# Local attention layers on one core: V shifted inside SBUF, key blocks paired by row half, a new order of the slot

## The chip, the cores and the metric

The kernel runs on one core of one Trainium2 chip. The metric is the device time in microseconds (us), as the median over runs; lower is better. Engines are named as in the profile: PE is TensorE's matmuls, PEld its weight loads, DVE is VectorE, ACT is ScalarE, POOL is GpSimd and SP is SyncE, whose queue issues the DMAs.

## The reference

Input `x` has 4 sequences of 512 tokens with 128 features. First comes one dense causal attention layer with 16 heads of 64, which the change leaves alone. Then a stack of 6 layers follows; each is local attention and a feed-forward part:

```python
def attn_layer(x, Wqkv, qs, ksc, Wo):
    q, k, v = split_heads(x @ Wqkv)          # 16 heads of 64
    q, k = l2norm(q) * qs, l2norm(k) * ksc   # t / max(|t|, 1e-12)
    q, k = rotary(q, scale), rotary(k, 1 / scale)
    out = local_attention(q, k, v)           # window 32
    return merge_heads(out) @ Wo
def local_attention(q, k, v):
    # tokens in blocks of 32; block j attends to key blocks j-1 and j, masked
    sim = einsum('bhwie,bhwje->bhwij', bq, bk2) * 8
    attn = softmax(where(mask, -max, sim), -1)
    return einsum('bhwij,bhwje->bhwie', attn, bv2)
def ffn_layer(x, g, bln, W1, b1, W2, b2):
    a, gate = split((layernorm(x, eps=1e-5) * g + bln) @ W1 + b1)
    return a * gelu(gate) @ W2 + b2
```

Each half of a layer takes the tokens with half of the features shifted by one token, and adds its result to `x`. So a query block of 32 tokens needs the keys and values of 64 tokens: its own block and the one before.

## The kernel before

The dense layer fills the first 571 us of the profiled execution. The 6 local layers are then cut into 96 units: 6 layers x 4 sequences x 4 tiles of 128 tokens (`NT` = 4). A unit has `NW` = 4 query blocks of `W` = 32 tokens. Heads are handled in pairs: `NC` = 8 pairs, and a pair is two heads h = 0, 1 of `HD` = 64.

The units are software pipelined. One call of `slot(n)` works on several of them: `u` is unit n (scores, softmax, attention times V), `prev` is unit n-1 (output projection and residual), `done` is unit n+1 (norms of q and k, their transposes, loading of V), `new` is unit n+2 (projection of k and of V, rotary products) and `newq` is unit n+3 (projection of q). All of it stands under `tc.manual_schedule()`: on each engine the instructions run in the order in which the functions are called, and semaphores are set between engines by what is read and written. The feed-forward part of a finished sequence is spread over the following slots by n modulo 4: type 0 has the hidden chunk 1 (`chunk`, L828 and L829), type 1 the mean of the layer norm (L100) and chunk 2, type 2 the variance (L109), the reciprocal root (`rsqrt`, L81 to L87) and the output `out` (L848), type 3 the scaling (L117), the affine step (L123, DVE) and chunk 0.

The order on PE in a slot before is: `scores` (L711 adds the mask band, L722 the products), `pair_sums` (L620), `project_out_2` (L784), the piece of the layer norm, the first half of k's projection (L547), `transpose_p` half 0 (L700), the second half of k's projection, `transpose_p` half 1, `times_v` halves 0 and 1 (L759), `project_v` (L562), the feed-forward chunk or output, q's projection (L547), and `transpose_o` (L700). DVE has `maximum` (L735), `guard` (L624), the two rotary products of q (L602, tiles `rot` and `t`), `residual` (L792), `sum_squares` of q (L596), then for each half of `times_v` the reciprocal L768 and the product L769, the transposes of q and k (L677, L685), the two rotary products of k (L602), `sum_squares` of k, and the gate of the chunk (L836). ACT has the exponentials (L743, 8 for each half), `seed` (L628, L629) between the halves, the copies of P's transposes (L703), `square` of k (L586), the copies of V (L569), gelu (L832) with the loading of its table, the loading of the first table again (L1005), `square` of q and the copies of `transpose_o` (L703). POOL has `newton`, `over_norm` (L640) and `add_rotated` (L614).

PSUM tiles: three of 2 banks each go round between the scores, the two halves of `times_v`, the projections of q and k, and the feed-forward chunk (`two_t`); two of one bank go round among the rest (`one_t`). The chunk takes the tile that half 1 of `times_v` had, so it waits for the product L769 that reads it.

A matmul here may use a part of the array: `scores` and `times_v` use tiles of 64 rows by 32 columns, so a pair of heads can take the upper and the lower row half at once, and four query blocks the four column groups. In the kernel before, row half h holds head h of the pair, and writes PSUM bank h; query block j writes the partitions 32j to 32j+31. For that, V of a head has to lie in the row half of its head, with the two key blocks of a query block side by side. So `project_v` stores V to DRAM (L574, `vd<-vt`), and two slots later `load_v` reads it back four times in that arrangement (L692, `vw<-vd`):

```python
rows = vd_rows(u, odd * W, P).rearrange("(j k) a x -> a k j x", k=2 * W)
...
    out=u.vw[c * HD : (c + 1) * HD, odd::2].rearrange("p j c d -> p j (c d)"), in_=rows[c]
```

Of the kernel before, what the change touches and what calls it, by code (L numbers as in the profile page):

```python
# [15 lines left out]
P = 128  # L16
# [16 lines left out]
def body(ctx: ExitStack, tc: tile.TileContext, a, out: bass.AP):  # L33
# [15 lines left out]
    small = ctx.enter_context(tc.tile_pool(name="small", bufs=4))  # L49
    dram = ctx.enter_context(tc.tile_pool(name="dram", bufs=1, space=bass.MemoryType.DRAM))  # L50
    def tmpt(n=S):
# [23 lines left out]
    def rsqrt(v, n, eng):  # L75
# [7 lines left out]
        for k in range(3):  # L83
# [3 lines left out]
            eng.tensor_tensor(y if k < 2 else v, y, t, ALU.mult)  # L87

    def layernorm_steps(state, bank, inT, outT, g=None, b=None, eng=nc.vector, nt=NT, temp=tmpt, later=None):

        w = nt * P

        def then(f):
            f() if later is None else later.append(f)

        def mean():
            m = bank()[:, 0:w]
            mm(m, lhsT=avg, rhs=inT(), start=True, stop=True)  # L100
            xc = state["xc"] = temp()[:, 0:w]
            nc.vector.tensor_tensor(xc, inT(), m, ALU.subtract)
            sq = state["sq"] = temp()[:, 0:w]
            then(lambda: nc.scalar.activation(sq, xc, AF.Square))

        def var():
            v = bank()
            for t in range(nt):
                mm(v[:, t : t + 1], lhsT=state["sq"][:, t * P : (t + 1) * P], rhs=avg[:, 0:1], start=True, stop=True)  # L109
            rs = state["rs"] = small.tile([P, NT], F32, tag="rs", name="rs")[:, 0:nt]  # L110
            nc.vector.tensor_scalar(rs, v[:, 0:nt], EPS, None, ALU.add)
            then(lambda: rsqrt(rs, nt, eng))

        def scale():
            bc = bank()[:, 0:w]
            for t in range(nt):
                nc.tensor.transpose(  # L117
                    bc[:, t * P : (t + 1) * P], state["rs"][:, t : t + 1].to_broadcast([P, P]), ident
                )
            h = state["h"] = outT()  # L120
            nc.vector.tensor_tensor(h, state["xc"], bc, ALU.mult)
            if g is not None:
                then(lambda: nc.vector.tensor_scalar(h, h, g, b, ALU.mult, ALU.add))  # L123

        return mean, var, scale
# [369 lines left out]
    ps = ctx.enter_context(tc.tile_pool(name="ps2", bufs=1, space=PSUM))  # L495
    s2a = ps2a = s2b = s2 = ps_one = vts = vds = None

# [60 lines left out]
    def project_v(u):  # L558
        vt = vts[u.n % 2]
        for g in range(2):  # L560
# [12 lines left out]
        used(u, 2)  # L573
        nc.sync.dma_start(out=vd_rows(u, W, P), in_=vt.rearrange("p a c d -> p a (c d)"))  # L574

    def vd_rows(u, first, n):
        r0 = u.T * P + first
        return vds[u.n // NT % 2][r0 : r0 + n]

# [74 lines left out]
    def second_step():  # L654

        nonlocal s2b, ps_one, vts, vds
        steps[1].close()
# [3 lines left out]

        vts = [s2b.tile([P, 2, NC, HD + 1], F32, tag=f"vt{j}", name=f"vt{j}") for j in range(2)]
        for t_ in vts:
            nc.gpsimd.memset(t_[:, :, :, HD : HD + 1], 1.0)
        vds = [dram.tile([W + S, 2, NC * (HD + 1)], F32, tag=f"vd{j}", name=f"vd{j}") for j in range(2)]
        for d_ in vds:
            nc.sync.dma_start(out=d_[0:W], in_=a["zeros"])

# [17 lines left out]

    def load_v(u):
        u.vw = s2b.tile([P, NW, NC, HD + 1], F32, tag="vw", name="vw", bufs=2)
        for odd in range(2):
            rows = vd_rows(u, odd * W, P).rearrange("(j k) a x -> a k j x", k=2 * W)  # L690
            for c in range(2):
                nc.sync.dma_start(  # L692
                    out=u.vw[c * HD : (c + 1) * HD, odd::2].rearrange("p j c d -> p j (c d)"), in_=rows[c]
                )

    def transposed(src, g, dst, col0):
# [6 lines left out]
        nc.scalar.copy(dst[:, 4 * g : 4 * g + 4, col0 : col0 + P], tp.rearrange("p (c t) -> p c t", c=4))  # L703

    def scores(u):

        sc = two_t(0, "ps_att")
        for j in range(NW):
            for h in range(2):
                rows = slice(h * HD, (h + 1) * HD)  # L710
                mm(  # L711
                    sc[j * W : (j + 1) * W, h, :],
                    lhsT=ident16[rows, h * HD : h * HD + W],
                    rhs=band[rows, min(u.T + j, 1)].unsqueeze(1).to_broadcast([HD, NC, 2 * W]),
                    start=True,
                    stop=False,
                    skip_group_check=True,
                )
        for c in range(NC):
            for j in range(NW):  # L720
                for h in range(2):
                    mm(  # L722
                        sc[j * W : (j + 1) * W, h, c * 2 * W : (c + 1) * 2 * W],
                        lhsT=u.qT[h * HD : (h + 1) * HD, j, c],
                        rhs=u.kT[h * HD : (h + 1) * HD, j : j + 2, c],
                        start=False,
                        stop=True,
                        skip_group_check=True,
                    )
        u.sc = sc  # L730
# [21 lines left out]
    def times_v(u, g):  # L752
        if g == 0:
            u.on = s2.tile([P, NC, 2, HD], F32, tag="on", name="on", bufs=1)
        o = two_t(g, "ps_att")
        for c in range(4):
            for j in range(NW):
                for h in range(2):
                    mm(  # L759
                        o[j * W : (j + 1) * W, h, c * (HD + 1) : (c + 1) * (HD + 1)],  # L760
                        lhsT=u.pT[h * HD : (h + 1) * HD, 4 * g + c, j * W : (j + 1) * W],
                        rhs=u.vw[h * HD : (h + 1) * HD, j, 4 * g + c, :],
                        start=True,
                        stop=True,
                    )
        ov = o[:, :, 0 : 4 * (HD + 1)].rearrange("p a (c d) -> p a c d", d=HD + 1)
        rden = small.tile([P, 2, 4, 1], F32, tag="rden", name="rden")
        nc.vector.reciprocal(rden, ov[:, :, :, HD : HD + 1])  # L768
        nc.vector.tensor_tensor(  # L769
            u.on[:, 4 * g : 4 * g + 4].rearrange("p c a d -> p a c d"),  # L770
            ov[:, :, :, 0:HD],
            rden.to_broadcast([P, 2, 4, HD]),
            ALU.mult,
        )

    def transpose_o(u):
        u.aT = s2.tile([P, NC, P], F32, tag="aT", name="aT", bufs=2)
        for g in range(2):
            transposed(u.on.rearrange("p c a d -> p (c a d)"), g, u.aT, 0)

    def project_out_2(u):
        y = u.y = one_t()
        for c in range(NC):
            mm(y[:, 0:P], lhsT=wo_w[0][:, c, :], rhs=u.aT[:, c, :], start=(c == 0), stop=(c == NC - 1))  # L784

# [140 lines left out]
    def slot(n, norm, move, geglu):  # L926
# [5 lines left out]
        if ends and new.T == 0:  # L932
            scales[0] = load_scales(new.i + 1)
        if done:
            load_v(done)
        if u:
            scores(u)
        if done:
            pair_sums(done)
        begin(unit(n + 4))  # L940
        if u:
            maximum(u)
        if done:
            guard(done)
        if u:
            exponents(u, 0)
        if done:
# [7 lines left out]
        if prev:  # L955
            project_out_2(prev)
            if prev.b + 1 == B and prev.T + 1 == NT and prev.i + 1 < L:
                wo_w[0] = load_wo(prev.i + 1)
        if new:
            rotate(new, 0, [lambda: residual(prev)] if prev else ())  # L960
        elif prev:
            residual(prev)
# [8 lines left out]
        if new:  # L971
            sum_squares(new, 0)
            add_rotated(new, 0)
            project(new, 1, k_tile, 0, 1)
        if u:
            transpose_p(u, 0)
        if new:
            project(new, 1, k_tile, 1)
        if u:
            transpose_p(u, 1)  # L980
        if new:
            square(new, 1)
        if u:
            times_v(u, 0)
            times_v(u, 1)
        while later:
            later.pop(0)()
        if done:
            transpose_q(done)
            transpose_k(done)  # L990
        if new:
            rotate(new, 1)
            add_rotated(new, 1)
            sum_squares(new, 1)
            project_v(new)
        if ends:
# [3 lines left out]
        if n == -1:  # L1000
            third_step()
        if newq:
            project(newq, 0, q_tile)
        if geglu and unit(n + 1):
            nc.scalar.preload_act_table_set("natural_log_exp_and_others")  # L1005
        if newq:
            square(newq, 0)
        if u:
            transpose_o(u)

# [108 lines left out]
def _constants(n):  # L1119
# [40 lines left out]
    ident16 = np.eye(P).astype(ml_dtypes.bfloat16)  # L1160
    zeros = np.zeros((W, 2, NC * (HD + 1)), f)
    return {"tabs": tabs, "band": band, "pen": pen, "ident16": ident16, "zeros": zeros, "pairs": pairs}
# [55 lines left out]
```

## Time and profile before

| | |
|---|---|
| median of 3 runs | 2262.44 us (2252.24 to 2264.42) |
| profiled execution: its own time | 2257.68 us |
| its span (first to last instruction) | 2255.9 us, mean granted PE clock 0.982 |
| dense layer / 96 slots and the end | 0 to 571 us / 571 to 2255.9 us |
| the 95 slots from the first to the last start | 571.0 to 2206.7 us, mean 17.2 us |
| busy: PE / DVE / ACT / POOL | 2108.4 / 1705.3 / 1457.2 / 1374.0 us |
| DMA: `vw<-vd` / `vd<-vt` | 384 of 260 KB / 96 of 520 KB |
| DMA of instructions (q8) | 309 packets, 5.06 MB |

A line of the page's groups reads: source line, engine, operation, output tile <- input tiles, shape, count, then busy time and mean duration in ns, and after the bar the idle time of the engine just before, with what ended most of it. "issue" stands for idle time in which the engine waited for nothing that the profile shows. In a timeline each row gives start and duration in us. The granted clock (PEclk) is 1.00 at full speed.

### The profile page before, as it was taken

How to read it: one execution, taken by the hardware profiler on the slowest of the kernel's cores; microseconds unless marked ns; L12 is line 12 of the kernel's file. 1: busy time of each engine (PE TensorE's matmuls, PEld its weight loads, DVE VectorE, ACT ScalarE, POOL GpSimd, SP SyncE). 2: the span in 40 equal slices, each digit the busy share in tenths (PEclk: the TensorE clock that was granted, in tenths of full speed). 3: DMA queues.
4: the chain of work that ended last, by engine and by line, in shares of the span. 5: the costliest groups of instructions: out<-in, count | busy, mean ns of one | idle time of the engine just before them, and what ended most of it. 6: DMA issues, size and time to landing. Idle time of an engine off the chain costs nothing.

```text
span 2255.9 us, 88566 instructions
## 1 busy us (share of the span) xinstructions
PE 2108.4 (93%) x39182; PEld 1338.7 (59%) x39182; DVE 1705.3 (76%) x2402; ACT 1457.2 (65%) x3860; POOL 1374.0 (61%) x1582
## 2 busy tenths in 40 slices
PE   7999999998898899989999999999889998999997
PEld 5655656554565556655566655666555665566665
DVE  4776767665787788877888877888778887878883
ACT  4665656664556667756677756777666776667763
POOL 2544545464666666766667666676666676666752
PEclk8999999999999999999999999999999999999998
DMA  3000000001343344333443424343343433434330
GB/s 122 1 1 1 1 1 1 1 1 29 88 117 88 89 124 118 93 92 89 125 117 106 109 82 117 103 116 99 98 114 98 116 99 98 114 89 115 101 101 23
DMA packets 88987, 180.35 MB, mean 80 GB/s; under 512 B 9342, under 2 KB 23548, under 8 KB 88572
## 3 DMA queue, kind: packets, MB, share of 16 engines
q1 hardware_dynamic: 87900, 172.98, 28.1%
q8 instruction: 309, 5.06, 1.0%
q10 hardware_dynamic: 704, 1.70, 0.2%
q14 instruction: 74, 0.61, 0.1%
HBM read 122.48 MB, written 52.43 MB: 78 GB/s over the span
## 4 chain that ended last, share of the span: by engine, by line
PE 78%; DVE 11%; ACT 5%; issue 4%; POOL 1%; DMA 0%; SPq 0%; DVEq 0%; ACTq 0%; POOLq 0%
PE ps_proj L547 13%; PE ps_one L700 7%; PE ps_one L784 6%; PE ps_att L759 6%; PE ps_att L722 6%; PE ps_one L562 6%; PE ps_sc L303 5%; PE ps_o L388 5%; PE ps_pt L368 4%; ACT pr L743 3%; PE ps_proj L828 3%; PE ps_proj L829 3%; DVE mx L735 2%; PE ps_att L711 1%; PE ps_proj L848 1%
## 5 line engine op out<-in xcount | busy, mean ns | idle before, releaser
L614 POOL TENSOR_TENSOR rot<-rot,t 128x1024 f32<-128x1024 f32 x192 | 457.4, 2382 | 225.6 <-DVE t L602 215.1
L743 ACT ACTIVATE pr<-ps_att,mx 128x64 f32<-128x64 f32 x1536 | 333.1, 328 | 202.9 <-DVE mx L735 202.9
L547 PE MATMUL ps_proj<-wqkv,xs 128*32 128x256 f32 x6144 | 399.3, 388 | 4.9 <-DVE t L602 2.5
L357 POOL TENSOR_TENSOR pr<-pr,den 128x1024 f32<-128x1024 f32 x128 | 240.9, 1893 | 248.1 <-DVE den L354 238.3
L640 POOL TENSOR_TENSOR rot<-rot,v 128x1024 f32<-128x1024 f32 x192 | 363.2, 1913 | 7.5
L547 PEld LDWEIGHTS ps_proj<-wqkv,xs 128*32 128x32 f32 x6144 | 172.5, 110 | 211.0 <-issue 120.0
L586 ACT ACTIVATE sq<-ps_proj 128x1024 f32<-128x1024 f32 x192 | 197.3, 1028 | 73.3 <-PE ps_proj L547 71.3
L602 DVE TENSOR_TENSOR t<-ps_proj,lt 128x1024 f32<-128x1024 f32 x192 | 232.4, 1210 | 0.0
L596 DVE TENSOR_REDUCE ss<-sq 128x32 f32<-128x1024 f32 x192 | 231.2, 1204 | 0.0
L602 DVE TENSOR_TENSOR rot<-ps_proj,lt 128x1024 f32<-128x1024 f32 x192 | 230.2, 1199 | 0.0
L569 ACT COPY vt<-ps_one 128x512 f32<-128x512 f32 x192 | 113.3, 590 | 180.7 <-PE ps_one L562 180.7
L343 ACT ACTIVATE pr<-ps_sc,nm 128x128 f32<-128x128 f32 (+3 forms) x448 | 220.3, 509 | 11.8 <-DVE nm L330 8.6
L784 PE MATMUL ps_one<-aT,wo 128*128 128x128 f32 x1536 | 201.8, 285 | 17.9 <-issue 17.7
L330 DVE TENSOR_REDUCE nm<-ps_sc 128x2 f32<-128x1024 f32 x128 | 156.0, 1219 | 64.4 <-PE ps_sc L318 64.4
L759 PE MATMUL ps_att<-vw,pT 64*32 64x65 f32 x12288 | 160.0, 225 | 44.2 <-issue 40.5
L784 PEld LDWEIGHTS ps_one<-aT,wo 128*128 128x128 f32 x1536 | 186.8, 198 | 19.6 <-issue 19.3
L562 PE MATMUL ps_one<-wqkv,xs 128*128 128x512 f32 x384 | 192.2, 622 | 6.5 <-DVE aT L398 3.6
L768 DVE RECIPROCAL rden<-ps_att 128x8 f32<-128x8 f32 x192 | 39.2, 204 | 203.0 <-PE ps_att L759 203.0
L759 PEld LDWEIGHTS ps_att<-vw,pT 64*32 64x32 f32 x12288 | 135.3, 105 | 70.3 <-issue 57.0
L634 POOL TENSOR_TENSOR yt<-y 128x64 f32<-128x64 f32 x96 | 28.0, 292 | 241.6 <-ACT y L629 239.7
L735 DVE TENSOR_REDUCE mx<-ps_att 128x16 f32<-128x1024 f32 x96 | 117.5, 1224 | 75.6 <-PE ps_att L722 75.2
L703 ACT COPY pT<-ps_one 128x512 f32<-128x512 f32 x192 | 114.8, 605 | 80.7 <-PE ps_one L700 80.6
(169 smaller groups left out, 3968.4 us busy)
## 6 DMA issues: line engine op xcount, KB each, us to landing
vw<-vd SPq DMA_DIRECT2D x384, 260.0 KB, 5.0
vd<-vt SPq DMA_DIRECT2D x96, 520.0 KB, 2.7
wqkv<-in_wqkv_dram SPq DMA_DIRECT2D x18, 512.0 KB, 3.8
wo<-in_wo_dram SPq DMA_DIRECT2D x6, 512.0 KB, 5.2
w<-in_w_dram SPq DMA_DIRECT2D x6, 341.0 KB, 3.5
xr<-in_x_dram SPq DMA_DIRECT2D x3, 256.0 KB
w<-in_w_dram SPq DMA_DIRECT2D x12, 64.0 KB
out_dram<-tmp_t SPq DMA_DIRECT2D x3, 256.0 KB, 2.3
```

Of the source, the lines that this page charges most:

```text
L343: nc.scalar.activation(self.pr[:, h, cols], self.sc[:, h, cols], AF.Exp, bias=self.nm[:, part_, h : h + 1], accum_out=self.den[:, part_, h ...
L357: nc.gpsimd.tensor_tensor(self.pr, self.pr, self.den[:, 0].unsqueeze(2).to_broadcast([P, 2, S]), ALU.mult)
L547: mm(u.p[j][b_ * W : (b_ + 1) * W, w_ // 2, w_ % 2 * n : (w_ % 2 + 1) * n], lhsT=u.xs[:, t0 : t0 + W], rhs=wpart[j][:, b_ * n : (b_ + 1) * n],
L562: mm(p, lhsT=u.xs[:, u.T * P : (u.T + 1) * P], rhs=wpart[2][:, g * 512 : (g + 1) * 512], start=True, stop=True,)
L586: nc.scalar.activation(u.sq[j], u.p[j], AF.Square)
L596: nc.vector.tensor_reduce(u.ss[:, j * GROUPS : (j + 1) * GROUPS], groups(u.sq[j]), AX.X, ALU.add)
L602: nc.vector.tensor_tensor(out_.rearrange("p (w c d) -> p w c d", w=NW, d=W), u.p[j].rearrange("p (w c d) -> p w c d", w=NW, d=W), lts[u.T] ...
L614: nc.gpsimd.tensor_tensor(r, r, t1[:, :, ::-1], ALU.add)
L640: nc.gpsimd.tensor_tensor(groups(u.r[j]), groups(u.r[j]), u.v[:, j * GROUPS : (j + 1) * GROUPS].unsqueeze(2).to_broadcast([P, GROUPS, W]), ...
L743: nc.scalar.activation(u.pr[:, c, h], u.sc[:, h, c * 2 * W : (c + 1) * 2 * W], AF.Exp, bias=u.mx[:, h, c : c + 1])
L759: mm(o[j * W : (j + 1) * W, h, c * (HD + 1) : (c + 1) * (HD + 1)], lhsT=u.pT[h * HD : (h + 1) * HD, 4 * g + c, j * W : (j + 1) * W], rhs=u ...
L784: mm(y[:, 0:P], lhsT=wo_w[0][:, c, :], rhs=u.aT[:, c, :], start=(c == 0), stop=(c == NC - 1))
```

## The change

Nothing changes in the dense layer or in the numbers of matmuls. In the local layers:

- **Key blocks by row half.** `PLACES` gives for each query block j and head h a bank `j // 2` and partitions `(h ^ j // 2) * 64 + j % 2 * 32`. In `scores` a row half still holds one head, but the two row halves now write the same bank, in different partitions. In `times_v` row half x holds the key blocks of the query blocks whose result goes to bank x, so that an odd block finds its two key blocks in `vt` as it was projected, and an even one in a copy `vs` that lies 32 tokens later.
- **V.** The store to DRAM and the four loads give way to two DMAs within SBUF (`shift_v`, 96 and 32 rows, 0.5 MB in all) into one buffer `vs`, issued after `times_v` of the slot. `vt` has three buffers instead of two.
- **Order.** k's projection is made whole, straight behind `scores`; q's projection comes last, behind `transpose_o`; ACT copies `transpose_o` before it squares q. On DVE the first rotary product of q moves ahead of `guard`, and the first rotary product of k moves ahead of the reciprocals of `times_v`, the second staying behind the transposes.
- **Layer norm in the slots.** The reciprocal root takes its first guess from ACT (Ln, then Exp) with one correction step on POOL, instead of two operations on DVE and three steps on POOL. The affine step moves from DVE to ACT.
- `wo`'s rows are permuted on the host side of the weights' layout to the new order of `on` and `aT`.

The core of the diff:

```diff
+    def rsqrt_log(v, n, eng):
...
+        nc.scalar.activation(y, v, AF.Ln)
+        nc.scalar.activation(y, y, AF.Exp, scale=-0.5)
+        eng.tensor_tensor(t, y, y, ALU.mult)
+        eng.tensor_tensor(t, t, v, ALU.mult)
+        eng.tensor_scalar(t, t, -0.5, 1.5, ALU.mult, ALU.add)
+        eng.tensor_tensor(v, y, t, ALU.mult)
...
-                then(lambda: nc.vector.tensor_scalar(h, h, g, b, ALU.mult, ALU.add))
...
+                    later.append(lambda: nc.scalar.activation(h, h, AF.Identity, bias=b, scale=g))
...
-        nc.sync.dma_start(out=vd_rows(u, W, P), in_=vt.rearrange("p a c d -> p a (c d)"))
...
+    def shift_v(u):
+        u.vs = s2b.tile([P, 2, NC, HD + 1], F32, tag="vs", name="vs")
+        nc.sync.dma_start(out=u.vs[W:P], in_=vts[u.n % 3][0 : P - W])
+        nc.sync.dma_start(out=u.vs[0:W], in_=vts[(u.n - 1) % 3][P - W : P] if u.T else a["zeros"])
...
+    PLACES = [(j, h, j // 2, (h ^ j // 2) * HD + j % 2 * W) for j in range(NW) for h in range(2)]
...
     def times_v(u, g):
...
+            for j, h, x_, p0 in sorted(PLACES, key=lambda f: (f[0] % 2, f[1], f[2])):
+                rows = slice(x_ * HD, (x_ + 1) * HD)
+                mm(
+                    o[p0 : p0 + W, x_, c * (HD + 1) : (c + 1) * (HD + 1)],
+                    lhsT=u.pT[rows, 4 * g + c, p0 : p0 + W],
+                    rhs=(vts[u.n % 3] if j % 2 else u.vs)[rows, h, 4 * g + c, :],
...
     def slot(n, norm, move, geglu):
...
-        if done:
-            load_v(done)
         if u:
             scores(u)
+        if new:
+            project(new, 1, k_tile)
         if done:
             pair_sums(done)
         begin(unit(n + 4))
         if u:
             maximum(u)
+            exponents(u, 0)
+        if new:
+            rotate(new, 0, [lambda: guard(done)] if done else ())
+        elif done:
             guard(done)
-        if u:
-            exponents(u, 0)
...
             sum_squares(new, 0)
             add_rotated(new, 0)
-            project(new, 1, k_tile, 0, 1)
         if u:
             transpose_p(u, 0)
-        if new:
-            project(new, 1, k_tile, 1)
-        if u:
             transpose_p(u, 1)
         if new:
             square(new, 1)
+        between = []
         if u:
-            times_v(u, 0)
-            times_v(u, 1)
...
+            between = [lambda: times_v(u, 0), lambda: times_v(u, 1)]
+        between.append(lambda: [f() for f in later] and later.clear())
         if done:
-            transpose_q(done)
-            transpose_k(done)
+            between.append(lambda: shift_v(done))
+            between.append(lambda: transpose_q(done))
+            between.append(lambda: transpose_k(done))
         if new:
-            rotate(new, 1)
+            rotate(new, 1, between)
             add_rotated(new, 1)
             sum_squares(new, 1)
...
+        if u:
+            transpose_o(u)
         if newq:
             project(newq, 0, q_tile)
...
             square(newq, 0)
-        if u:
-            transpose_o(u)
```

## The prediction

> **What bounds the kernel now.** I read the page first: engines, DMA queues, chain.
>
> ```profile
> PE 2108.4 (93%) x39182; PEld 1338.7 (59%) x39182; DVE 1705.3 (76%) x2402; ACT 1457.2 (65%) x3860; POOL 1374.0 (61%) x1582
> q1 hardware_dynamic: 87900, 172.98, 28.1%
> q8 instruction: 309, 5.06, 1.0%
> PE 78%; DVE 11%; ACT 5%; issue 4%; POOL 1%; DMA 0%; SPq 0%; DVEq 0%; ACTq 0%; POOLq 0%
> ```
>
> PE is busy for 93% and carries 78% of the chain. The DMA has 0% of the chain: the trip of V through DRAM (most of q1) is on no path by itself. Second, the waits:
>
> ```profile
> DVE rden L768 <- PE ps_att L759: 203.0, 130, 5.3
> PE ps_att L759 <- issue: 40.5, 34, 1.7
> PE ps_att L711 <- DVE t L602: 21.9, 19, 4.0
> PE ps_one L784 <- issue: 17.7, 10, 3.1
> PE ps_proj L828 <- DVE hT L123: 7.4, 10, 1.0
> ```
>
> PE hardly waits for data: 21.9 us at a slot's start for k's second rotary product, 7.4 for the affine step. Larger are the stalls with nothing to wait for. Third, one such stall in windows (PE, PEld, DVE, ACT and POOL busy, then clock, DMA share, GB/s):
>
> ```profile
> 1291.50:1295.00 3.50, 3.50 (x153) 3.29 (x152) 2.46 (x5) 1.68 (x5) 1.68 (x1) 1.00 0.93 211
> 1295.00:1297.20 2.20, 0.46 (x5) 0.27 (x3) 1.00 (x1) 2.17 (x12) 0.17 (x1) 1.00 0.73 149
> 1297.20:1300.00 2.80, 2.80 (x21) 2.15 (x25) 2.44 (x4) 1.39 (x7) 2.47 (x5) 0.57 0.01 5
> ```
>
> This is the start of a slot: the scores run while `vw<-vd` fills the DMA (0.93), then PE stands for 1.74 us of the next 2.20, then the clock is 0.57. The long stalls all resume at the same place in PE's stream modulo 256 instructions, 1.25 to 1.5 us after a packet of q8 has landed; 79097 PE and PEld records over 309 packets is 256 each. So they are instruction fetches. The place wanders by some 14 instructions a slot. Fourth, an undisturbed slot of type 0, in the timeline (start 1472.1):
>
> ```profile
> 1478.94 1.16 ACT L703 COPY pT<-ps_one 128x512 f32<-128x512 f32 x2
> 1479.63 1.51 PE L759 MATMUL ps_att<-vw,pT 64*32 64x65 f32 x128
> 1480.00 1.03 ACT L586 ACTIVATE sq<-ps_proj 128x1024 f32<-128x1024 f32 x1
> 1480.53 0.21 DVE L768 RECIPROCAL rden<-ps_att 128x8 f32<-128x8 f32 x1 [1.55 <-PE ps_att L759]
> 1480.77 0.69 DVE L769 TENSOR_TENSOR on<-ps_att,rden 128x512 f32<-128x512 f32 x1
> 1481.38 0.20 DVE L768 RECIPROCAL rden<-ps_att 128x8 f32<-128x8 f32 x1
> 1481.61 0.69 DVE L769 TENSOR_TENSOR on<-ps_att,rden 128x512 f32<-128x512 f32 x1
> 1482.89 1.02 PE L828 MATMUL ps_proj<-hT,w 128*128 128x512 f32 x2
> ```
>
> Undisturbed slots last 15.5, 16.1, 17.7 (0.7 to 0.8 of it the wait at L711) and 15.8 us by type, 16.25 on average, 1544 for 95; measured are 1635.7. The 92 us between are fetch stalls: about 50 in `times_v` (some 40 slots), 40 after the scores (some 20 slots), and some 17 lost at half clock after these (8 slots, 34 us together), less what they cover of other waits.
>
> **The change, part by part.** PE's matmuls stay the same, so its work stays; what counts is where it stands.
>
> *k's rotary product ahead of the reciprocals.* DVE idles there (the 203.0 us), so the place looks free. But in the changed program this product waits for ACT's `square` of k, the other reader of the same PSUM tile, which stands behind the two copies of pT. Times within a slot of type 0: `square` ends at 8.9 (the timeline's 1480.00 + 1.03 - 1472.1), the product takes 1.2 (row of L602: 1199 ns), so DVE is at 10.1. Behind it are queued two reciprocals and two products: 1.77 from the first start to the last end in the undisturbed slot; end at 11.9. The feed-forward chunk reuses the PSUM tile that the last product reads, so PE waits until then; V's projection is done at 10.76. That is 1.15 us of idle PE. The other types: the copy of pT half 0 now starts only after `transpose_p` half 0 at a later place (PE does all of k first), `square` ends at 9.5, 9.5 and 9.15, the last product at 12.5, 12.4 and 12.1, against 11.45, 11.3 and 11.2: 1.1, 1.1, 0.9. Mean 1.06. In the 40 slots with a stall in `times_v` (mean 1.25) V's projection ends that much later and the wait is covered, but for some ten short stalls (+5). In the other 55: 55 x 1.06 = **+58**, with +5 together **+63**. Bounds: 0 if PE is late anyway, 95 x 1.06 = 101 if no stall covers it.
>
> *pT later.* k's second half no longer stands between the two transposes, so `times_v` waits for the first copy by 0.12 (type 2) and 0.13 (type 3): 24 x 0.25 = **+6** (0 to 14).
>
> *The wait at L711* goes: the second product of k still stands behind the transposes, but would end at about 16, and the slots of type 2 last until 18.8, as two DVE steps of the root (501 and 918 ns groups; 2.6 us in that slot) leave: **-22** (bounds 0 and -22). *The affine step on ACT* ends at 9.8 (`square`, then 0.65 by the 688 ns of gelu), over 1 us before chunk 0: **-7**.
>
> *V within SBUF.* The two DMAs are issued behind `times_v` and needed 13 us later; the nearest row, the 520 KB store, lands in 2.7 us. Hidden, at nothing; SP's wait for the end of `times_v` holds back only loads at layers' ends, and a miss would cost up to a slot's DMA, some 5 us, each. What is gained is the fetch: with `vw<-vd` running, q8's packets start 1.5 to 3.6 us after their place was reached; without, 0.8 to 1.1. The stalls after the scores cost 57 with their clock. But now k's 64 instructions stand in dense order behind the scores, where 18 slow ones stood: exposed are some 118 places instead of 54, so 44 slots instead of 20. Each costs between 0.3 (3.5 us from place to resumption against 3.2 of dense work) and 1.3 (the stalls in `times_v`, with an idle DMA). I take 0.8: 35 remain, without clock loss, since stalls in `times_v` show none: **-22** (bounds 0 and -44). The Trainium skill, "Runtime: NRT & Kernel Launch", section "Instruction fetch mechanics", says that the next 256 instructions are fetched during execution and that a crossing is mostly hidden. By it nothing is gained here and the sum below would be 22 us higher; the 40.5 us at L759, with an idle DMA, contradict it.
>
> *Row halves in one bank.* No row of before has two row halves writing one bank at once. Free is the nearest row: L547's four column tiles write one bank together at full rate. The other bound: they take turns. Scores issue 8 tiles in about 0.1 us and stream 0.05, so turns fit; the band (8 matmuls in 0.41 us) would double, less what overlaps, 0.37 x 95 = 35. I take **0**, with 0 to +35. The Trainium skill, "PSUM — Partial Sum Buffer", section "PSUM bank collisions raise a hardware error", quotes that different row tiles can't access the same bank at the same time. By it this edit costs the 35 us, if the hardware makes them take turns; no row here shows it.
>
> *At nothing:* `guard` behind the rotary product is done at 4.6, ACT asks for it at 4.75; the gate ends 1.1 us into the next slot, k's projection wants its tile at 1.75; `square` of q ends at 1.4, its reader starts at 3.1; Ln and Exp on ACT take 0.5 us in its idle time before V's copies. Covers are thin (0.15, 0.65, 1.7); a miss of 0.2 in each slot would be 19 us.
>
> Sum: 63 + 6 - 22 - 7 - 22 + 0 = **+18**, on the profiled execution's own 2257.68 about 2276; the median lies 4.8 us above that execution, so 2280.
>
> **Rivals.**
> 1. *Faster: the stalls after the scores vanish.* If the packets, freed from V's traffic, arrive in time, the whole 57 is gained: 35 more, 2245. For it: the stalls sit where the DMA is at 0.93. Against: 40 stalls with no traffic. The change is below before from a fetch gain of 40 on (63 + 6 - 29).
> 2. *Slower: row halves take turns*, +35: 2315. For it: nothing in the profile. Against: L547's tiles.
> 3. *Little comes of either:* idle time behind V's projection covers stalls that shift there, or the wait is halved (-18): 2262.
>
> **How the numbers follow.** The forecast has 45% (its own range 2262 to 2300, by the bounds of fetch), rival 1 30%, rival 2 15%, rival 3 10%. The range goes from 2228 (rival 1 with the bound of the wait at 46 instead of 63) to 2322 (rival 2 with its covers thin). Faster by over 0.5% (about what a measurement of this kernel can tell): rival 1, 0.30. Within: rival 3 and the forecast's lower end, 0.17. Slower: 0.53.
>
> **What would show it.** Right: PE's chunk waits for DVE `on` by about 1 us in over half of the slots; DVE's second product of the slot waits for ACT's `square`; DVE's 203.0 us at the reciprocals nearly go; the wait at the band goes; HBM reads fall by about 100 MB. Wrong: no wait at the chunk (the first term falls), a band above 0.7 us for 8 (rival 2), no stall or half clock after the scores (rival 1), or a wait of `times_v` for the shifted V.

## The result and the profile after

The changed kernel takes 2286.74 us (median of 4 runs, 2283.64 to 2292.06) against 2257.34 for the kernel before in the same call: ratio 1.0131, 95% interval 1.0089 to 1.0174. Its profiled execution takes 2283.64 us, with a span of 2281.8. The forecast was 2280, slower than before.

The page of the changed kernel: engines, first DMA queue, HBM, and the chain that ended last.

```profile
PE 2074.0 (91%) x39182; PEld 1334.7 (58%) x39182; DVE 1657.7 (73%) x2336; ACT 1489.9 (65%) x3926; POOL 1336.7 (59%) x1407
q1 hardware_dynamic: 34076, 70.46, 10.5%
HBM read 23.18 MB, written 1.05 MB: 11 GB/s over the span
PE 71%; DVE 13%; ACT 9%; issue 5%; POOL 1%; DMA 0%; SPq 0%; DVEq 0%; ACTq 0%; POOLq 0%
```

The queue moves 70 MB instead of 173, and every engine but ACT has less to do than before. Yet the time is longer, and the chain has gone from PE (78% to 71%) to DVE and ACT: PE waits for data. Its waits (total, times, longest, in us):

```profile
DVE rot L611 <- ACT sq L595: 129.3, 95, 6.7
PE ps_att L764 <- issue: 59.7, 35, 2.2
PE ps_proj L839 <- DVE on L774: 42.7, 38, 1.3
PE ps_proj L859 <- DVE on L774: 14.1, 14, 1.1
PE ps_att L717 <- DVE t L611: 9.8, 8, 3.4
DVE rden L773 <- PE ps_att L764: 3.8, 11, 0.6
```

DVE now stands for ACT's `square` in 95 slots (129.3 us), where it stood for the attention times V before (203.0, now 3.8), and the feed-forward waits for `on`: 42.7 + 14.1 = 57 us that were not there. The stalls in the attention times V (L764) have grown from 40.5 to 59.7 us. The wait at the band fell from 21.9 to 9.8. One undisturbed slot of type 0 (start 1412.8), from the timelines of ACT, DVE and PE:

```profile
1420.54 1.03 ACT L595 ACTIVATE sq<-ps_proj 128x1024 f32<-128x1024 f32 x1
1421.60 1.22 DVE L611 TENSOR_TENSOR rot<-ps_proj,lt 128x1024 f32<-128x1024 f32 x1 [1.56 <-ACT sq L595]
1423.81 0.69 DVE L774 TENSOR_TENSOR on<-ps_att,rden 128x512 f32<-128x512 f32 x1
1424.65 1.10 PE L839 MATMUL ps_proj<-hT,w 128*128 128x512 f32 x2 [1.08 <-DVE on L774]
```

This is the queue that the prediction described: `square` ends at 8.7 us of the slot, k's product at 10.0, two reciprocals and a product of `on` follow, the last product of `on` at 11.7, and the chunk starts at 11.8 after 1.08 us of nothing.

### The profile page after: what moved, and what is told of

Its sections match the earlier page's. It is cut to its first block, busy times and chain, and to the rows that moved or that the text cites. A ratio compares the mean times of both kernels' runs of the same rounds, so it can differ in the third digit from the quotient of the medians.

```text
span 2281.8 us, 87954 instructions
## 1 busy us (share of the span) xinstructions
PE 2074.0 (91%) x39182; PEld 1334.7 (58%) x39182; DVE 1657.7 (73%) x2336; ACT 1489.9 (65%) x3926; POOL 1336.7 (59%) x1407
## 4 chain that ended last, share of the span: by engine, by line
PE 71%; DVE 13%; ACT 9%; issue 5%; POOL 1%; DMA 0%; SPq 0%; DVEq 0%; ACTq 0%; POOLq 0%
PE ps_proj L561 14%; PE ps_one L795 6%; PE ps_att L727 5%; PE ps_sc L317 5%; PE ps_o L402 5%; PE ps_pt L382 4%; DVE on L774 4%; PE ps_one L576 3%; PE ps_one L786 3%; DVE rot L611 3%; ACT pr L748 3%; PE ps_proj L839 3%; PE ps_proj L859 3%; PE ps_att L764 3%; PE ps_proj L840 3%
## 5 line engine op out<-in xcount | busy, mean ns | idle before, releaser
L561 PE MATMUL ps_proj<-wqkv,xs 128*32 128x256 f32 x6144 | 383.5, 383 | 8.1 <-issue 7.5
L611 DVE TENSOR_TENSOR rot<-ps_proj,lt 128x1024 f32<-128x1024 f32 x192 | 234.1, 1219 | 129.3 <-ACT sq L595 129.3
L561 PEld LDWEIGHTS ps_proj<-wqkv,xs 128*32 128x32 f32 x6144 | 183.0, 110 | 145.1 <-issue 38.8
L357 ACT ACTIVATE pr<-ps_sc,nm 128x128 f32<-128x128 f32 (+3 forms) x448 | 220.6, 511 | 11.7 <-DVE nm L344 8.6
L576 PE MATMUL ps_one<-wqkv,xs 128*128 128x512 f32 x384 | 199.8, 643 | 7.4 <-DVE aT L412 3.6
L344 DVE TENSOR_REDUCE nm<-ps_sc 128x2 f32<-128x1024 f32 x128 | 155.9, 1218 | 64.4 <-PE ps_sc L332 64.3
L795 PE MATMUL ps_one<-aT,wo 128*128 128x128 f32 x1536 | 192.9, 279 | 0.4 <-DVE rs L122 0.3
L764 PE MATMUL ps_att<-vs,pT 64*32 64x65 f32 x6144 | 147.6, 225 | 37.7 <-issue 28.9
L764 PE MATMUL ps_att<-vt,pT 64*32 64x65 f32 x6144 | 152.2, 226 | 30.9 <-issue 30.9
L795 PEld LDWEIGHTS ps_one<-aT,wo 128*128 128x128 f32 x1536 | 179.4, 192 | 0.9 <-issue 0.6
L764 PEld LDWEIGHTS ps_att<-vs,pT 64*32 64x32 f32 x6144 | 122.1, 105 | 60.3 <-issue 34.3
L382 PEld LDWEIGHTS ps_pt<-ident,pr 128*128 128x128 f32 x1024 | 118.2, 142 | 61.6 <-issue 48.1
```

Of the source, the lines that this page charges most:

```text
L357: nc.scalar.activation(self.pr[:, h, cols], self.sc[:, h, cols], AF.Exp, bias=self.nm[:, part_, h : h + 1], accum_out=self.den[:, part_, h ...
L382: nc.tensor.transpose(pt[:, k * P : (k + 1) * P], self.pr[:, h, k * P : (k + 1) * P], ident)
L561: mm(u.p[j][b_ * W : (b_ + 1) * W, w_ // 2, w_ % 2 * n : (w_ % 2 + 1) * n], lhsT=u.xs[:, t0 : t0 + W], rhs=wpart[j][:, b_ * n : (b_ + 1) * n],
L576: mm(p, lhsT=u.xs[:, u.T * P : (u.T + 1) * P], rhs=wpart[2][:, g * 512 : (g + 1) * 512], start=True, stop=True,)
L611: nc.vector.tensor_tensor(out_.rearrange("p (w c d) -> p w c d", w=NW, d=W), u.p[j].rearrange("p (w c d) -> p w c d", w=NW, d=W), lts[u.T] ...
L764: mm(o[p0 : p0 + W, x_, c * (HD + 1) : (c + 1) * (HD + 1)], lhsT=u.pT[rows, 4 * g + c, p0 : p0 + W], rhs=(vts[u.n % 3] if j % 2 else u.vs) ...
```

## The experiments

"Gaps" below are PE's idle stretches of over 0.1 us, summed over the 95 slots by what PE does next. Each ratio is against the kernel before, with its 95% interval.

**The place of k's rotary product.** Three kernels. The first puts it back behind the transposes:

```diff
-            rotate(new, 1, between)
+            for f in between:
+                f()
+            rotate(new, 1)
```

> The changed kernel with one thing undone: both rotary products of k stand behind the transposes on DVE again, as before the change. Theory (the first product waits for ACT's square of k and holds back the reciprocals, so the feed-forward chunk waits for the product that frees its PSUM tile): the 57 us of PE waiting at the chunk for DVE's on (43 at L839, 14 at L859) fall under 5, and the time falls from 2287 to about 2235. Thin cover: DVE's last step, the gate, ends some 1.6 us into the next slot, where k's projection wants its tile, so up to 10 us may come back there. Rival (the idle PE time there comes from elsewhere, or other stalls take its place): 2275 or more.

Measured: 2234.54 us, ratio 0.9917 (0.9894 to 0.9941). No wait for `on` is left at the chunk, and the wait at the band is back:

```profile
PE ps_att L717 <- DVE t L611: 25.3, 19, 5.0
```

The second leaves it ahead of the attention times V, but calls `square` behind it:

```diff
-        if new:
-            square(new, 1)
         between = []
+        if new:
+            between.append(lambda: square(new, 1))
         if u:
-            between = [lambda: times_v(u, 0), lambda: times_v(u, 1)]
+            between += [lambda: times_v(u, 0), lambda: times_v(u, 1)]
```

> The changed kernel with ACT's square of k called behind DVE's first rotary product of k instead of ahead of it, so that the product waits only for PE and the square for the product. Theory: DVE makes the product between 7.2 and 9.7 us of the slot, on is ready before V's projection ends, the wait at the chunk falls under 5 us in all; ACT's square ends up to 1 us later, which its readers have room for. Time about 2230, below the kernel before. Rival (two readers of one PSUM tile are not what matters, the product is simply too long for that place): the wait at the chunk stays above 30 us and the time above 2265.

Measured: 2222.93 us, ratio 0.9857 (0.9833 to 0.9880). The gaps at the chunk fall from 57 us to 0.3. The rival is refuted: the product fits there, it is the wait for the other reader that doesn't. Three waits of this kernel, for the last experiment below: PE stands in the attention times V for nothing and for the copy of P's transposes, and at these transposes for DVE:

```profile
PE ps_att L764 <- issue: 55.8, 34, 2.2
PE ps_att L764 <- ACT pT L707: 5.9, 26, 0.7
PE ps_one L704 <- DVE tmp_t L113: 10.0, 23, 0.4
```

The third kernel adds the product's new place to the kernel before:

```diff
-            times_v(u, 0)
-            times_v(u, 1)
-        while later:
-            later.pop(0)()
...
-            rotate(new, 1)
+            rotate(new, 1, between)
```

> The kernel before with one thing of the change added: the first rotary product of k ahead of the attention times V on DVE. Theory: it waits for ACT's square of k here too, and the chunk waits about 1 us in the slots without a stall: 45 to 60 us at L828 and L848 for DVE's on, time 2295 to 2315. Rival (DVE's idle time there was free): 2257 or, with the wait at the band gone, 2240.

Measured: 2342.47 us, ratio 1.0391 (1.0357 to 1.0425), more than the theory's upper end. The waits at the chunk and the output:

```profile
PE ps_proj L828 <- DVE on L769: 29.6, 28, 1.2
PE ps_proj L828 <- DVE hT L123: 25.3, 16, 2.6
PE ps_proj L848 <- DVE on L769: 13.3, 12, 1.2
```

The wait for `on` is there, and with the affine step still on DVE, queued behind the same product, chunk 0 waits up to 2.6 us for that (7.4 us in all before). So the product behind `square` costs 88 us in the order of before, and its undoing gains 48 (the product back behind the transposes) or 62 (ahead of `square`).

**V.** The kernel before with the new places of the key blocks and V shifted in SBUF; order and layer norm as before:

```diff
-        if done:
-            load_v(done)
         if u:
             scores(u)
...
         if done:
+            shift_v(done)
             transpose_q(done)
```

(with `PLACES`, `times_v`, `transpose_o`, `project_v` and the order of `wo` as in the change)

> The kernel before with the new places of the key blocks and V shifted within SBUF alone; order of the slot and the layer norm as before. Theory (V's trip through DRAM delays instruction fetches after the scores, about 35 us of stalls there and some 7 us at half clock): the stalls after the scores fall by 20 to 35 us, the time falls from 2257 to 2225 to 2240. If the arrangement of V itself makes the stalls within the attention times V longer (68 us in the changed kernel, 44 before), they are 68 here too and the time is 2245 to 2260; if the order of the slot does, they stay at 44. Rival (the traffic was hidden): 2257, stalls after the scores as before.

Measured: 2195.65 us, ratio 0.9731 (0.9710 to 0.9753), a gain of 61 us, beyond the theory's best. The stalls of the attention times V and behind the scores:

```profile
PE ps_att L761 <- issue: 32.2, 26, 1.9
PE ps_att L714 <- DVE t L608: 22.6, 21, 4.0
PE ps_one L792 <- issue: 3.7, 5, 1.3
```

Between the first and the last slot's start 62.5 us are saved: 28 of stalls from the scores to the transposes (L784 alone from 17.7 to 3.7), 8 in the attention times V, 10 at half clock (22.0 to 11.9 us lost), and 9 because the scores themselves end at 1.68 us of the slot and not at 1.78, their median; the remaining 8 are spread.

Is it the amount of traffic, or where it lies? The first attempt called the loads later:

```diff
-        if done:
-            load_v(done)
         if u:
             scores(u)
...
         if done:
+            load_v(done)
             transpose_q(done)
```

> The kernel before with one thing changed: V still goes through DRAM in the same DMAs, but the four loads are issued behind the attention times V of the slot instead of at its start. Theory (what costs is that this traffic runs while PE is in the dense scores and fetches its instructions): the stalls after the scores fall as with V alone, scores take 0.15 us less a slot, time 2195 to 2215. Rival (the amount of traffic matters, wherever it runs, or the gain of V alone came from V's arrangement on the array): above 2240.

Measured: 2261.96 us, ratio 1.0050 (1.0031 to 1.0069). It tells nothing: SP has nothing to wait for ahead of the loads and issues them as early as before. The mean DMA share in the first four us of a slot is 0.56, 0.82, 0.88, 0.83 (before 0.51, 0.83, 1.02, 0.99). The second, with the loads called there too, gives the loaded V one buffer, so that they wait for the end of the attention times V:

```diff
-        u.vw = s2b.tile([P, NW, NC, HD + 1], F32, tag="vw", name="vw", bufs=2)
+        u.vw = s2b.tile([P, NW, NC, HD + 1], F32, tag="vw", name="vw", bufs=1)
```

> The kernel before with one buffer for the loaded V instead of two, its loads called behind the attention times V: now they wait for the end of that (in the run before, e6_v_loads_later, SP issued them as early as ever, since nothing held them, and the DMA share over the slot stayed as it was). So the same 1.56 MB a slot move, but none beside the scores. Theory (place in time matters: traffic beside the dense scores delays fetches and slows the scores' matmuls): stalls behind the scores fall from 35 us to under 10, scores end at 1.69 instead of 1.78 us, time 2195 to 2220. Rival (the amount matters, or the gain of V alone lies in its arrangement): 2245 or more, stalls behind the scores unchanged or moved to another place of the slot.

Measured: 2251.57 us, ratio 1.0005 (0.9989 to 1.0020). Now the traffic lies at 11 to 18 us from the slot's start, so its tail still runs beside the next slot's scores (mean DMA share in their first us 0.74, before 0.51, then 0.29). The scores end at 1.68 in the median, and the stalls behind them fall, but they come up in the scores. Its waits, then a slot that starts at 945.1 (windows; clock, DMA share and GB/s last):

```profile
PE ps_att L722 <- issue: 38.5, 24, 3.0
PE ps_one L784 <- issue: 9.4, 8, 1.9
```

```profile
941.10:945.10 4.00, 4.00 (x43) 1.95 (x41) 4.00 (x4) 3.94 (x5) 2.12 (x3) 1.00 1.06 251
945.10:946.80 1.70, 1.69 (x136) 1.45 (x135) 0.94 (x2) 1.42 (x3) 1.62 (x1) 1.00 0.62 230
946.80:948.80 2.00, 0.00 (x1) 0.00 (x1) 0.00 (x0) 0.00 (x0) 0.00 (x0) 1.00 0.00 0
948.80:951.00 2.20, 2.20 (x13) 2.13 (x14) 1.92 (x3) 0.67 (x4) 0.00 (x0) 0.70 0.04 7
```

The DMA is full before the slot, PE then stands for 2 us in which no packet starts, and the clock falls. The theory's 2195 to 2220 is missed. The first half of the rival fits, the amount: 1.56 MB a slot keep the DMA busy for 6 to 7 us in both places, and the instructions due in that time come late. All 43 stalls of over 1 us that wait for nothing resume here at one place of PE's stream modulo 256, as do 38 of 38 before and 21 of 22 in V alone, and the median packet of the instruction queue starts 1.56 us after PE reached that place one block earlier in the kernel before, 1.11 here and 0.93 in V alone (in the slots). The other half, V's arrangement, is not settled: no run has it with the old traffic, so its share of the 61 us is not shown. In V alone 0.52 MB lie at 10 to 13 us, beside V's projection and the chunk, where few instructions last long.

**The layer norm.** V alone, with the root's first guess and the affine step on ACT:

```diff
-            then(lambda: rsqrt(rs, nt, eng))
+            then(lambda: (rsqrt if later is None else rsqrt_log)(rs, nt, eng))
...
-                then(lambda: nc.vector.tensor_scalar(h, h, g, b, ALU.mult, ALU.add))
+                    later.append(lambda: nc.scalar.activation(h, h, AF.Identity, bias=b, scale=g))
```

> V alone (the run before: 2196) with the change's layer norm added (first guess of the root by ACT's logarithm, affine step on ACT), order of the slot as before the change. Theory: what is left on DVE there is the wait of the band for k's second product (22.6 us in 21 slots) and of chunk 0 for the affine step (7 us); both go: about 2170, at least 2180. Rival (the idle time there covers other waits, stalls take its place): 2190 to 2200.

Measured: 2163.62 us, ratio 0.9605 (0.9579 to 0.9631): 28 us (0.0126 of 2255), a little more than expected. The gaps at the band fall from 19.5 to 10.2 us without the first slot, at the chunk from 8.4 to 0, and half clock costs 5 us less (11.9 to 6.6). With the first slot, the wait at the band is:

```profile
PE ps_att L717 <- DVE t L611: 13.3, 9, 4.0
```

**The order.** V alone with k's projection whole behind the scores:

```diff
             scores(u)
+        if new:
+            project(new, 1, k_tile)
...
-            project(new, 1, k_tile, 0, 1)
...
-        if new:
-            project(new, 1, k_tile, 1)
```

> V alone (2196) with one part of the change's order added: k's projection whole and straight behind the scores. Theory: this order, not V's arrangement, makes the stalls within the attention times V longer and adds waits at the transposes of P (64 and 16 us in the changed kernel with the product of k first, against 37 and 0 in V alone): 60 to 65 and 15 here, time 2225 to 2240. Rival (q's projection behind the transposes of the output, or the moves on DVE, do it): 2200 or less.

Measured: 2322.75 us, ratio 1.0291 (1.0248 to 1.0335): far worse than expected. Gaps: attention times V 58, transposes of P 49, band 31, chunk 25, k's projection 15. The direction of the theory is right, the size is not. `pair_sums` now stands behind k's projection as well, and in this kernel `guard`, which waits for it, is still ahead of q's products on DVE: DVE stands there for 1.4 us a slot (in V alone for 5.9 us once). The output projection comes 1.9 us later and the residual 1.7, POOL's norms are 1.7 later in slots of type 0, DVE's transposes 2.2 in the median, and the band waits. The change, which puts `guard` behind q's first product, has 17.0 us of that wait. And the affine step falls beside POOL's sum (its source line, min/median/max ns; in V alone the median is 808):

```profile
DVE v L630 <- PE ps_one L626: 131.4, 95, 7.7
L134 DVE TENSOR_SCALAR hT<-hT,vecs x25: 348/2259/2667, 709.5 to 2307.6; 128x512 f32<-128x512 f32 x23, 128x384 f32<-128x384 f32 x1, 128x128 f32<-128x128 f32 x1
```

V and norm, with q's projection last:

```diff
-        if newq:
-            project(newq, 0, q_tile)
...
         if u:
             transpose_o(u)
+        if newq:
+            project(newq, 0, q_tile)
+            square(newq, 0)
```

> V and norm (2164) with one part of the change's order added: q's projection behind the transposes of the output, and ACT's square of q behind their copies. Theory (the change's order costs through k's projection, which delays the output projection, the residual and so POOL's chain to the norms): nothing here, 2155 to 2175. Rival (q's projection right ahead of the scores makes fetch stalls): 2185 or more, with stalls in the scores and behind them.

Measured: 2157.55 us, ratio 0.9584 (0.9557 to 0.9612): this part costs nothing. V and norm, with k's first product ahead of the attention times V and of `square` (the edit of e2_rk_first, made there):

> V and norm (2164) with the first rotary product of k moved into DVE's idle time ahead of the attention times V, called ahead of ACT's square so that it doesn't wait for it. Theory: DVE ends each slot 1.2 us earlier; the wait of the band (10 us, 4 of them once at the start) is all there is to gain: 2155 to 2163. If the square, now behind the product, comes too late for V's copies, or the product holds back the reciprocals: 2170 or more.

Measured: 2160.00 us, ratio 0.9599 (0.9576 to 0.9623), as expected; not told apart from V and norm. An attempt to shorten the stalls in the attention times V, on V and norm:

```diff
             square(new, 1)
+            project_v(new)
         if u:
             times_v(u, 0)
             times_v(u, 1)
+        if newq:
+            project(newq, 0, q_tile)
```

> V alone with the layer norm, and V's projection ahead of the attention times V, q's projection right behind it and ahead of the feed-forward chunk. If stalls within the attention times V arise because its 256 instructions run faster than the next 256 come in, then four long matmuls ahead of it give the fetch 1.8 us more, and the stalls (37 us) fall by half or more: 2150. If they don't depend on what stands ahead, about 2170 as with V and norm alone. If on ends too late for the chunk or pT too late for nothing to cover it, above 2180.

Measured: 2300.61 us, ratio 1.0208 (1.0178 to 1.0238). The stalls hardly change (35.2 to 33.2 us, fewer and longer), so four long matmuls ahead don't help the fetch, and new waits come up, the largest at the band:

```profile
PE ps_att L717 <- DVE t L611: 56.9, 63, 3.2
PE ps_att L764 <- issue: 32.9, 27, 2.3
```

Last, all of the change, with `square` behind the product, and k's projection in halves and `guard` as before:

```diff
-        if new:
-            project(new, 1, k_tile)
...
+            project(new, 1, k_tile, 0, 1)
         if u:
             transpose_p(u, 0)
+        if new:
+            project(new, 1, k_tile, 1)
+        if u:
             transpose_p(u, 1)
```

> Everything of the change, with the first rotary product of k called ahead of ACT's square (as in e2_rk_first, 2223), but k's projection in two halves around the first transposes of P as before, and with it guard ahead of q's rotary product. Theory: k's projection straight behind the scores is what costs the 60 us between e2_rk_first and the two runs at 2158 to 2160, since it puts off the output projection by 1.9 us, and what hangs on it, and leaves nothing but weight loads and short matmuls ahead of the attention times V: here 2150 to 2160, stalls within the attention times V 35 us as against 64. Rival (the parts add up differently): 2170 or more.

Measured: 2157.03 us, ratio 0.9547 (0.9522 to 0.9571), the lowest ratio of all and 4.5% below the kernel before. Its engines and waits:

```profile
PE 2063.7 (96%) x39182; PEld 1327.5 (62%) x39182; DVE 1644.4 (76%) x2336; ACT 1488.2 (69%) x3926; POOL 1335.7 (62%) x1407
PE ps_att L764 <- issue: 31.7, 25, 1.9
PE ps_att L717 <- DVE t L611: 5.6, 2, 3.0
```

It differs from e2_rk_first by k's place and by the order on DVE that goes with it: `guard` ahead of q's first product, and the residual, as in the kernel before, between q's two products. In the change `guard` stands between them and the residual behind both. Together this costs 0.9857 - 0.9547, 70 us. By gaps the slots lose 28 in the attention times V (35.9 to 64.3; 5 of it the wait for the copy of pT, 0.9 to 5.9), 16 at the transposes of P (0 to 15.8; 14.5 of it waits for DVE's steps of the layer norm, L113 and L132), 10 at k's projection, and 22 at half clock (5.1 to 27.3), 76 for a difference of 75.

The change as a ladder, each step added to those above:

| step | ratio to before | step, us of 2255 |
|---|---|---|
| V in SBUF, key blocks by row half | 0.9731 | -61 |
| layer norm's root and affine step | 0.9605 | -28 |
| q's projection last, k's product ahead of `square` | 0.9547 | -13 |
| k's projection whole behind the scores, with its order on DVE | 0.9857 | +70 |
| k's product behind `square` (the change) | 1.0131 | +62 |

By the intervals of the ratios a step is uncertain by 5 to 11 us, so -13 is hardly clear of it; in the traces the 95 slots fall from 1541.7 to 1530.0 us there.

## Why the prediction was right, and where it was not

The direction and the size came out (+18 forecast, +29 measured). The largest term came out by the mechanism that was named; that the rest came close is in part luck. V and k's place were forecast at -22 + 6 = -16 and measured at -61 + 70 = +9, and the -13 of the ladder's third step, which the sum did not have, made up for half of that.

- **k's product behind `square`: right.** Forecast +63, ladder +62. Forecast 1.06 us in 55 slots, measured 57 us at L839 and L859 in 52 gaps, 1.09 each; forecast end of `on` 11.9, measured 11.7 in the slot of type 0 shown. Its undoing (e1_rk_behind, e2_rk_first) and its addition (e4_before_rk_ahead) show it from both sides.
- **V: the term was mis-sized.** The forecast -22 is net of what k's place would expose. Of the 57 for the stalls behind the scores, the prediction's price of 0.8 for each of 20 slots would leave 16 in V alone: -41. Measured: -61. The step that failed is "44 slots instead of 20, 0.8 each": it counted exposed places by density and took the stalls with an idle DMA for the price. With V alone 5 us of gaps are left from the scores to the transposes (33 before), the stalls in the attention times V shrink too, and the scores end 0.1 us earlier, which the sum had not at all. The Trainium skill, "Runtime: NRT & Kernel Launch", "Instruction fetch mechanics", calls the crossings mostly hidden; V alone (32.2 us at L761) and e9_v_loads_after_av (38.5 at L722) show them to cost tens of us, and the second shows them to move with the traffic. (The resumption after a packet's landing, given as 1.25 to 1.5 us, reaches 1.61 in the trace of before.)
- **k's projection early: the other mis-sized term.** Forecast +6 as "pT later" and, of the fetch term, 24 more exposed slots at 0.8, +19; measured +70. The +6 nearly came out: 5.8 us in 26 waits in the changed kernel (0.9 before). The step that failed is where the fetches would be exposed: they were sought behind the scores, and the stalls in the attention times V were taken as unchanged. From e14_all_but_k_early to e2_rk_first k's projection gains 10 us of gaps, but the stalls in the attention times V grow from 31.7 to 55.8, with 22 at half clock behind them; and the transposes of P wait for the layer norm, which k's first half had kept apart from them. "Stalls in `times_v` show none" held for before (up to 1.71 us), not beyond: half clock follows four of the five stalls of 1.68 to 1.94 us there in V alone, and in the changed kernel seven of its nine stretches at half clock begin in or behind a stall of 1.76 to 2.18 us there, while eleven others of 1.77 to 2.20 us are not followed by it. Why those stalls are longer with k early is open: e10_v_norm_spread speaks against the simple picture that long matmuls ahead shorten them.
- **Layer norm: right in sum.** Forecast -22 - 7, ladder -28. But at the band only 9 of the 22 came, 10 us are left there (5.6 of the waits with k's product ahead as well); the affine step's 7 came (8), 5 are half clock, and the rest is spread.
- **Row halves in one bank: 0, as taken.** The band's matmuls have a median of 386 ns in both kernels, the products' 216, and the scores end at 1.68 us with the old places (e9_v_loads_after_av) and with the new (V alone). So no turns are seen; the rule on row tiles that the Trainium skill quotes ("PSUM — Partial Sum Buffer", "PSUM bank collisions raise a hardware error") cost no time in this edit.
- **The covers held, but for the thinnest:** ACT waits for `guard` (L637 for L633) 7.5 us in 18 slots, all others not at all; k's projection doesn't wait for the gate, and the shifted V is waited for 0.2 us in all.

Rival 1 (the stalls behind the scores vanish) is right in its mechanism: they nearly do with V alone, and in the changed kernel the gaps at both projections of q and k come to 7.7 us where 35 were taken. It did not come true in the sum, since k's place cost more elsewhere.

## What to carry to other kernels

A hole on an engine's row is free only if the work put there is ready: look at which other reader or writer of the same PSUM tile the program lets go first, and what stands in the queue behind. A transfer with 0% of the chain can still cost, through the instruction fetches that come late beside it; take it away alone and see before mixing it with a new order. A step moved on PE moves everything that its result starts on the other engines, so follow it to the end of their queues.

## What the hardware showed that was not expected

**A DVE step beside POOL.** On DVE the root's steps on 128x4 elements take 0.17 us alone and up to 2.3 beside POOL. The timelines of the kernel before, DVE and POOL:

```profile
1514.57 2.28 DVE L82 TENSOR_SCALAR y<-yt 128x4 int32<-128x4 int32 x1
1514.47 2.35 POOL L614 TENSOR_TENSOR rot<-rot,t 128x1024 f32<-128x1024 f32 x1
```

The step ends 0.03 us after POOL's sum. Of the 77 steps of the root and the affine step behind the dense layer in that trace, 37 are long (root over 0.3 us, affine over 1.0), and all 37 end 0.03 us (root) or 0.5 us (affine) after a POOL operation that was running when they began. The Trainium skill, "SBUF — State Buffer", section "SBUF: two separate sides", tells of a port pair that DVE and POOL share as an exclusive lock; the trace agrees. The rotary products (L602), which read PSUM, lie between 1.18 and 1.22 us whatever POOL does. So a small step of this kind on DVE costs what POOL happens to be doing. How much of the layer norm's 28 us this is, no run separates.

**The scores' end, and traffic.** The scores end at a median of 1.78 us of the slot before and at 1.68 in V alone and in e9_v_loads_after_av. A busy DMA by itself doesn't explain it: in e9_v_loads_after_av 14 slots without a stall in the scores have a DMA share of over 0.9 from 0.85 to 1.70 us, and they end at 1.68 as well, while the 16 slots of before with a share under 0.3 there have 1.75. The cause is open.
